# Softplus of the time steps: one VectorE sum out of the bank, the bias as a matmul row, dt written by VectorE

## The chip, the cores and the metric

The kernel runs on one core of one Trainium2 chip. The metric is the device time of one execution in microseconds, as the median of three runs. A profiled execution of the same kernel gives the trace that the sections below read. The engines are called PE (TensorE, with PEld for its weight loads), DVE (VectorE), ACT (ScalarE), POOL (GpSimd) and SP (SyncE, which issues nearly all DMAs here).

## The reference

The input is x of shape (4, 384, 32, 32) in float32: four images, 384 channels, 1024 positions. Two layers follow.

Layer 0 normalises x by groups of channels and runs a selective scan in four directions k (by rows, by columns, and both backwards). For each direction:

```python
dts = jnp.einsum('bkrl,kdr->bkdl', x_dbl[:, :, :R], dt_projs_weight)      # R = 12
dt = jax.nn.softplus(dts + dt_projs_bias[None, :, :, None])
# per position, for each of the 16 states n:
h = h * jnp.exp(dt[..., None] * A) + (dt * u)[..., None] * B
y = einsum(h, C)
```

The four results and a skip term are added up, normalised over channels, put through gelu and added to x. Layer 1 is attention over 1024 positions with a causal window of 64 (six heads of 64), then a mixture of four experts, two per position, with hidden size 1536. All of it is in float32.

The change concerns softplus and the product dt * u. With z = dts + bias and e = exp(-|z|), softplus(z) is max(z, 0) + log(1 + e). The kernel computes the logarithm with a correction for the rounding of w = 1 + e: it takes c = (w - 1) - e and uses log(w) - c.

## The kernel before

**Tiles and turns.** Channels are cut into T = 3 parts of 128 partitions. A turn is one image and one direction: 16 turns. In a turn, each third of the channels has one time step tile of 128 x 1024, so there are 48 steps. For the scan, each third is cut again into four blocks of 32 channels, and each block, with 4 states side by side, gives four tiles of 128 x 1024 called slots: 768 slots in all.

**A slot.** ACT writes the decay dA = exp(dt * A) into PSUM (`decay`, two buffers of two banks). POOL multiplies dt * u by B into z (`times_b`, seven buffers). DVE runs the scan over dA and z (`scan`). The product with C is made on POOL or on DVE (`times_c`), whichever the written order says is less loaded. PE folds the four states into a sum in a PSUM bank (`fold_y`). Attention (`tokens`), routing (`route`) and experts (`experts`, `combine`) of finished images run beside the scan of later ones; what is left of them runs after the last scan.

**Order.** All instructions are written ahead of time. `Machine.run` (line 335) steps through generators such as `time_steps` and `scan`, prices every operation with a simple model (`Engine.ask`, line 154) and appends it to the order of its engine. On the chip each engine runs its own list in that order, and waits where an operand isn't there. Shared buffers are `Stock`s; taking one can have to wait. For PSUM there are the two dA buffers, one bank for the experts' output and the stock `banks` of only three banks (line 471), which everything else shares by rank: 0 for the time steps and the folds, 1 by default, 2 for the experts' hidden layer. `copy` (line 561) puts a copy out of a bank on DVE or ACT, whichever modelled clock is behind.

**A time step before** (`time_steps`, line 741). It may run up to 40 slots ahead of the scan. SP loads u. Two banks are taken, one for each half of 512 columns, and PE multiplies `dtw_sb` (12 rows of weights) by `xd` (12 rows). The halves use rows 0 to 11 and 32 to 43, which `turn_loads` (line 717) has loaded for the turn with two DMAs each. ACT then makes Abs into e and Relu into dt, both with the per-partition bias `dtb_sb`, and the banks are given back. ACT makes Exp over all 1024 columns of e. Two banks are taken anew, and ACT writes w = 1 + e into them. DVE makes c in e. ACT makes Ln in place in the bank. For each half DVE subtracts c, adds dt (both in place in the bank) and multiplies by u into e. ACT copies the bank to dt, and the bank is given back. SP writes e and dt to DRAM (`dtr`), from where `spread` loads them, each row four times over. For directions 1 and 3 the multiply reads u by columns.

The tiles u, e and dt are 128 x 1024 each in SBUF; e and dt have one buffer each, so the next step waits for their DMAs.

Of the kernel before, what the change touches and what calls it, by code (L numbers as in the profile page):

```python
# [11 lines left out]
F32 = mybir.dt.float32  # L12
AF = mybir.ActivationFunctionType
ALU = mybir.AluOpType
# [3 lines left out]
P = 128  # L18
B, D, HH, WW = 4, 384, 32, 32
L = HH * WW  # L20
T = D // P
HB = 512
NH = L // HB
KG, NS, R = 4, 16, 12
# [42 lines left out]
def colmajor(ap):  # L67

    return ap.rearrange("p (h w) -> p w h", w=WW)
# [307 lines left out]
def conv_attn_hybrid(  # L377
# [7 lines left out]
    nc = tc.nc  # L385
    const = ctx.enter_context(tc.tile_pool(name="const", bufs=1))
    dram = ctx.enter_context(tc.tile_pool(name="dram", bufs=2, space=bass.MemoryType.DRAM))

    def const_load(src, shape, name):
        dst = const.tile(shape, F32, name=name)  # L390
        nc.sync.dma_start(dst, src)
        return dst

    xw_sb = const_load(xw, [P, T, KG, XR], "xw_sb")
    dtb_sb = const_load(dtb, [P, KG, T], "dtb_sb")
    ds_sb = const_load(ds_, [P, KG, T], "ds_sb")
    lnw_sb = const_load(lnw, [P, T], "lnw_sb")
    lnb_sb = const_load(lnb, [P, T], "lnb_sb")
# [72 lines left out]
    banks = Stock(m, ps_b, "ps", 3, [P, HB])  # L471
# [4 lines left out]
    with tc.tile_pool(name="setup", bufs=1) as setup:  # L476
# [15 lines left out]
        for j in range(JB):  # L492
            ps = banks.now("ps_al")
# [15 lines left out]
    work = ctx.enter_context(tc.tile_pool(name="work", bufs=1))  # L509
# [42 lines left out]
    pe, act, dve, pool, sp = m.pe, m.act, m.dve, m.pool, m.sp  # L552
# [65 lines left out]
    def group_norm(b):  # L618
# [68 lines left out]
        def project(pair):  # L687
            xos = yield from zs_.take("xo", n=2)
            for h in range(NH):
                us = yield from us_.take("ux", n=2)  # L690
                uv = [us[t // NH][:, ts(t % NH, HB)] for t in range(T)]
                for t in range(T):
                    yield from sp.dma_start(uv[t], udr[b][t][:, ts(h, HB)])
                ps = yield from banks.take("ps_x", 0)
                pv = ps[: 2 * XR, :]
                mm = Calls()
                for t in range(T):
                    mm.matmul(
                        pv, xw_sb[:, t, 2 * pair : 2 * pair + 2, :].rearrange("p k r -> p (k r)"),
                        uv[t], start=t == 0, stop=t == T - 1,  # L700
                    )
                yield from pe.all(mm)
                us_.give(*us)
                yield from act.copy(xos[0][: 2 * XR, ts(h, HB)], pv)
                yield from copy(
                    xos[1][: 2 * XR, :].rearrange("r (w h) -> r h w", h=HH)[:, ts(h, HH // NH), :],
                    pv.rearrange("r (h w) -> r h w", w=WW),
                )
                banks.give(ps)
            for n in (1, 0):  # L710
                yield from sp.dma_start(xdr[b][2 * pair + n], xos[n][n * XR : (n + 1) * XR, :])
                have.add(("x", b, 2 * pair + n))
            zs_.give(*xos)

        yield from m.together([project(pair) for pair in (0, 1)], 2 if b == 0 else 1, EARLY)

    def turn_loads():
        for i, (b, k) in enumerate(turns):
            yield lambda: ("x", b, k) in have and (i == 0 or (i - 1, T - 1) in dtrs)

            xd = work.tile([32 + R, HB], F32, tag="xd", name="xd")
            dtw_sb = work.tile([32 + R, D], F32, tag="dtw", name="dtw_sb")
            for h in range(NH):
                r = slice(32 * h, 32 * h + R)
                yield from sp.dma_start(xd[r], xdr[b][k, :R, ts(h, HB)])
                yield from sp.dma_start(dtw_sb[r], dtw[:, k])
            xds[i], dtws[i] = xd, dtw_sb

    def state_rows(c):
# [11 lines left out]
    def time_steps():  # L741

        for i, (b, k) in enumerate(turns):
            for t in range(T):
                yield lambda: i in xds and ("u", b) in have and count_of["scan"] >= (i * T + t) * TS - 40
                u = yield from us_all.take("ub")
                yield from sp.dma_start(u, udr[b][t])


                e = work.tile([P, L], F32, tag="e", name="e")  # L750
                dt = work.tile([P, L], F32, tag="dt", name="dt")
                bias = dtb_sb[:, k, t : t + 1]
                pss = []
                for h in range(NH):
                    pss.append((yield from banks.take("ps_dt", 0)))
                mm = Calls()
                for h in range(NH):
                    r = slice(32 * h, 32 * h + R)
                    mm.matmul(pss[h], dtws[i][r, ts(t, P)], xds[i][r], start=True, stop=True)
                yield from pe.all(mm)  # L760
                for h, ps in enumerate(pss):
                    c = ts(h, HB)
                    yield from act.activation(e[:, c], ps, AF.Abs, bias=bias)
                    yield from act.activation(dt[:, c], ps, AF.Relu, bias=bias)
                    banks.give(ps)
                yield from act.activation(e, e, AF.Exp, scale=-1.0)

                ws = []
                for h in range(NH):
                    w = yield from banks.take("ps_sp", 0)  # L770
                    yield from act.activation(w, e[:, ts(h, HB)], AF.Identity, bias=1.0)
                    ws.append(w)
                for h, w in enumerate(ws):
                    c = ts(h, HB)
                    yield from dve.scalar_tensor_tensor(e[:, c], w, -1.0, e[:, c], ALU.add, ALU.subtract)
                for w in ws:
                    yield from act.activation(w, w, AF.Ln)
                for h, w in enumerate(ws):
                    c = ts(h, HB)
                    yield from dve.tensor_tensor(w, w, e[:, c], ALU.subtract)  # L780
                    yield from dve.tensor_tensor(w, w, dt[:, c], ALU.add)
                    if k % 2:
                        v = slice(h * (WW // NH), (h + 1) * (WW // NH))
                        yield from dve.tensor_tensor(
                            e[:, c].rearrange("p (w h) -> p w h", h=HH),
                            w.rearrange("p (w h) -> p w h", h=HH), colmajor(u)[:, v, :], ALU.mult,
                        )
                    else:
                        yield from dve.tensor_tensor(e[:, c], w, u[:, c], ALU.mult)
                    yield from act.copy(dt[:, c], w)  # L790
                    banks.give(w)
                us_all.give(u)
                dtr = dram.tile([2, P, L], F32, tag="dtr", name="dtr", bufs=4)
                yield from sp.dma_start(dtr[1], e)
                yield from sp.dma_start(dtr[0], dt)
                dtrs[i, t] = dtr
# [679 lines left out]
    with tc.manual_schedule():  # L1476
        for b in range(B):
            m.spawn(group_norm(b), EARLY)
        for gen in (turn_loads(), time_steps(), state_rows(0), state_rows(1), spread(1), spread(0)):
            m.spawn(gen, EARLY)  # L1480
        for gen in (decay(), times_b(), scan()):
            m.spawn(gen)
        m.spawn(layer1(), EARLY)
        for gen in (prepare(), mixture()):
            m.spawn(gen, LATER)
        m.run()
# [54 lines left out]
```

## Time and profile before

| What | us |
| --- | --- |
| median of three runs | 4074.07 (4067.94 to 4078.49) |
| profiled execution, its own time | 4065.49 |
| its span | 4063.8 |
| POOL's first z product starts | 95.7 |
| last scans end (VectorE's list of instructions in order of time) | about 3140 |
| DVE / POOL / ACT / PE busy in the span | 2878.0 / 2855.7 / 2432.7 / 3014.8 |
| ACT table loads, 388 of 1283 ns | 497.8 |

In the profile's groups, a line names the engine, the operation, "out<-in" with the program's tile names (`ps_dt` and `ps_sp` are the banks of a time step, `ub` is u), the shapes and the count; then busy time, mean length in ns, idle time of the engine just ahead of it and what ended that idle time. L141 and L152 are the helper lines that issue single operations and lists of them, so groups are told apart by tile. In the waits, "A x <- B y: 10.0, 5, 3.0" says that engine A stood still 10.0 us ahead of x, 5 times, at most 3.0 us, until B had made y.

### The profile page before, as it was taken

To read this page: it belongs to the slowest core of one execution; us is meant where nothing else is said; L and a number is where in the kernel's file an instruction comes from. 1 tells how busy PE (TensorE), PEld (TensorE's weight loads), DVE (VectorE), ACT (ScalarE), POOL (GpSimd) and SP (SyncE) were. 2 spreads that over 40 slices of the span, in tenths; PEclk is the share of its full clock that TensorE was granted. 3 is DMA by queue.
4 is the path that set the end of the run, shared out by engine and by line. 5 is a ranking of instruction groups with operands and counts; after the bars stand their busy time and mean duration, and the time that the engine had idled before them with its cause. 6 is when DMAs were issued, how large, how long until landed. Compare 5 with 4: busy or idle time off the path is not lost. (4 is left out here: it accounts for less than half of the span.)

```text
span 4063.8 us, 49234 instructions
## 1 busy us (share of the span) xinstructions
PE 3014.8 (74%) x15856; PEld 1854.0 (46%) x15856; DVE 2878.0 (71%) x3064; ACT 2432.7 (60%) x3979; POOL 2855.7 (70%) x1490
## 2 busy tenths in 40 slices
PE   3554455576674888677777786767799999998998
PEld 1000000043441455445454444444466788887886
DVE  2999999998889888888888889888897232101001
ACT  3554455476774798777776787877777345222221
POOL 1999989989897789999987899899997110101001
PEclk8555566577775899878877787887799999998997
DMA  5565564634345989464668795664569754998995
GB/s 200 203 250 209 217 209 151 209 109 162 114 154 184 382 315 355 164 229 140 215 209 283 268 358 195 230 197 171 190 243 337 240 170 142 345 335 295 315 317 193
DMA packets 368570, 935.11 MB, mean 230 GB/s; under 512 B 48372, under 2 KB 160120, under 8 KB 368312
## 3 DMA queue, kind: packets, MB, share of 16 engines
q1 hardware_dynamic: 360120, 906.79, 63.6%
q0 software_dynamic: 8192, 25.17, 1.8%
q8 instruction: 126, 2.06, 0.2%
q14 instruction: 132, 1.08, 0.1%
HBM read 786.39 MB, written 164.30 MB: 234 GB/s over the span
## 5 line engine op out<-in xcount | busy, mean ns | idle before, releaser
L141 POOL TENSOR_TENSOR z<-dts,bc 128x1024 f32<-128x1024 f32 x768 | 1792.2, 2358 | 177.7 <-PE ps_y L152 95.3
L141 ACT ACTIVATE dA<-dts,a 128x1024 f32<-128x1024 f32 x768 | 851.1, 1116 | 485.5 <-DVE z L141 456.6
L152 PE MATMUL ps_y<-z,fold 128*32 128x512 f32 x3072 | 734.9, 806 | 536.1 <-POOL z L141 253.6
L141 DVE TENSOR_TENSOR_SCAN dA<-dA,z 128x1024 f32<-128x1024 f32 x393 | 899.1, 2288 | 107.6 <-ACT dA L141 88.6
L141 POOL TENSOR_TENSOR z<-z,bc 128x1024 f32<-128x1024 f32 x375 | 879.6, 2356 | 102.6 <-DVE z L141 99.7
L141 DVE TENSOR_TENSOR_SCAN z<-dA,z 128x1024 f32<-128x1024 f32 x375 | 843.8, 2276 | 41.2 <-ACT dA L141 39.4
L152 PEld LDWEIGHTS ps_hid<-xbt,w_sb 128*128 128x128 f32 x5472 | 682.1, 201 | 132.5 <-issue 25.7
L152 PE MATMUL ps_hid<-xbt,w_sb 128*128 128x128 f32 x5472 | 702.0, 286 | 38.0 <-ACT dt L141 19.4
L152 PE MATMUL y_ff<-w_sb,hs 128*128 128x384 f32 x1824 | 659.7, 500 | 19.2 <-ACT hs L141 15.2
L141 ACT ACTIVATE hs<-ps_hid,bb 128x128 f32<-128x128 f32 x912 | 270.5, 366 | 457.1 <-PE ps_hid L152 351.6
L152 PEld LDWEIGHTS ps_y<-z,fold 128*32 128x32 f32 x3072 | 95.1, 123 | 971.4 <-POOL z L141 466.2
L141 ACT ACT_TABLE_LOAD x388 | 497.8, 1283 | 17.2 <-issue 3.6
L141 DVE TENSOR_TENSOR z<-dA,bc 128x1024 f32<-128x1024 f32 x393 | 479.8, 1221 | 13.0
L152 PEld LDWEIGHTS y_ff<-w_sb,hs 128*128 128x128 f32 x1824 | 331.7, 195 | 240.5 <-issue 47.5
L141 POOL DMA_INDIRECT cb<-ysdr,idx x64 | 61.7, 963 | 441.6 <-issue 281.7
L141 DVE COPY xbt<-ps_xb 128x384 f32<-128x384 f32 x39 | 21.7, 556 | 407.7 <-PE ps_xb L152 407.7
L152 POOL TENSOR_TENSOR rn<-rn,half 128x1 f32<-128x1 f32 x96 | 52.5, 547 | 265.6 <-DVE rn L152 256.2
L141 POOL DMA_INDIRECT xsdr<-tks,idx x64 | 63.9, 999 | 168.9 <-DMA xsdr<-tks,idx 119.5
L152 PE MATMUL ps_dt<-xd,dtw_sb 12*128 12x512 f32 x192 | 99.8, 856 | 45.9 <-ACT dt L141 19.2
L152 PE MATMUL ps_o<-v,pt 128*128 128x64 f32 (+1 forms) x720 | 110.1, 315 | 19.6 <-DVE tt L141 7.2
L141 ACT COPY dt<-ps_sp 128x512 f32<-128x512 f32 x96 | 56.0, 584 | 113.5 <-DVE e L141 113.2
L152 PEld LDWEIGHTS ps_o<-v,pt 128*128 128x128 f32 (+1 forms) x720 | 104.9, 227 | 29.4 <-DVE tt L141 7.7
(189 smaller groups left out, 3219.4 us busy)
## 6 DMA issues: line engine op xcount, KB each, us to landing
w_sb<-wl SPq DMA_DIRECT2D x608, 576.0 KB
dts<-dtr SPq DMA_DIRECT2D x384, 512.0 KB
bc<-xdr SPq DMA_DIRECT2D x128, 512.0 KB
ub<-udr SPq DMA_DIRECT2D x48, 512.0 KB
dtr<-e SPq DMA_DIRECT2D x48, 512.0 KB
dtr<-dt SPq DMA_DIRECT2D x48, 512.0 KB
yp<-ydr SPq DMA_DIRECT2D x96, 256.0 KB
ydr<-yp SPq DMA_DIRECT2D x96, 256.0 KB
```

The source lines that it names most:

```text
L141: return getattr(self.real, op)(*a, **k)
L152: getattr(self.real, op)(*a, **k)
```

## The change

z with its bias comes ready out of the matmul, and dt never passes through a bank on its way out.

- The bias becomes a 13th row of the weights, against a row of ones. `xd` is one constant tile, set to 1.0 once, of which the turns overwrite rows 0 to 11 and 32 to 43. Twelve small DMAs at the start lay the bias out in DRAM (`dtbr`), and each turn loads its row twice. `dtb_sb` is gone.
- ACT makes Abs of both halves without a bias, then Exp. There is no Relu.
- DVE makes max(z, 0) + e out of the bank into dt in one instruction.
- ACT writes w = 1 + e over z in the same bank; no second pair of banks is taken. The two banks are held from the matmul to the last subtraction.
- DVE makes (w - 1) - (max(z, 0) + e) in e, ACT makes Ln in place, and DVE subtracts: dt = log(w) - e goes straight to SBUF. The bank is given back there.
- The multiply by u reads dt from SBUF in place of w in the bank. ACT's copy to dt is gone.

```diff
-    dtb_sb = const_load(dtb, [P, KG, T], "dtb_sb")
...
+    xd = const.tile([32 + R + 1, HB], F32, name="xd")
+    nc.vector.memset(xd, 1.0)
+    dtbr = dram.tile([KG, D], F32, name="dtbr", bufs=1)
+    for k in range(KG):
+        for t in range(T):
+            nc.sync.dma_start(dtbr[k, ts(t, P)].unsqueeze(1), dtb[:, k, t : t + 1])
+
     def turn_loads():
...
-            xd = work.tile([32 + R, HB], F32, tag="xd", name="xd")
-            dtw_sb = work.tile([32 + R, D], F32, tag="dtw", name="dtw_sb")
+            dtw_sb = work.tile([32 + R + 1, D], F32, tag="dtw", name="dtw_sb")
             for h in range(NH):
                 r = slice(32 * h, 32 * h + R)
                 yield from sp.dma_start(xd[r], xdr[b][k, :R, ts(h, HB)])
                 yield from sp.dma_start(dtw_sb[r], dtw[:, k])
+                yield from sp.dma_start(dtw_sb[32 * h + R : 32 * h + R + 1, :], dtbr[k : k + 1, :])
...
-                bias = dtb_sb[:, k, t : t + 1]
...
-                    r = slice(32 * h, 32 * h + R)
+                    r = slice(32 * h, 32 * h + R + 1)
...
                 for h, ps in enumerate(pss):
+                    yield from act.activation(e[:, ts(h, HB)], ps, AF.Abs)
+                yield from act.activation(e, e, AF.Exp, scale=-1.0)
+                for h, ps in enumerate(pss):
                     c = ts(h, HB)
-                    yield from act.activation(e[:, c], ps, AF.Abs, bias=bias)
-                    yield from act.activation(dt[:, c], ps, AF.Relu, bias=bias)
+                    yield from dve.scalar_tensor_tensor(dt[:, c], ps, 0.0, e[:, c], ALU.max, ALU.add)
+
+                for h, ps in enumerate(pss):
+                    yield from act.activation(ps, e[:, ts(h, HB)], AF.Identity, bias=1.0)
+                for h, ps in enumerate(pss):
+                    c = ts(h, HB)
+                    yield from dve.scalar_tensor_tensor(e[:, c], ps, -1.0, dt[:, c], ALU.add, ALU.subtract)
+                for ps in pss:
+                    yield from act.activation(ps, ps, AF.Ln)
+                for h, ps in enumerate(pss):
+                    c = ts(h, HB)
+                    yield from dve.tensor_tensor(dt[:, c], ps, e[:, c], ALU.subtract)
                     banks.give(ps)
-                yield from act.activation(e, e, AF.Exp, scale=-1.0)
-
-                ws = []
-                for h in range(NH):
-                    w = yield from banks.take("ps_sp", 0)
-                    yield from act.activation(w, e[:, ts(h, HB)], AF.Identity, bias=1.0)
-                    ws.append(w)
-                for h, w in enumerate(ws):
-                    c = ts(h, HB)
-                    yield from dve.scalar_tensor_tensor(e[:, c], w, -1.0, e[:, c], ALU.add, ALU.subtract)
-                for w in ws:
-                    yield from act.activation(w, w, AF.Ln)
-                for h, w in enumerate(ws):
-                    c = ts(h, HB)
-                    yield from dve.tensor_tensor(w, w, e[:, c], ALU.subtract)
-                    yield from dve.tensor_tensor(w, w, dt[:, c], ALU.add)
...
-                            w.rearrange("p (w h) -> p w h", h=HH), colmajor(u)[:, v, :], ALU.mult,
+                            dt[:, c].rearrange("p (w h) -> p w h", h=HH), colmajor(u)[:, v, :], ALU.mult,
...
-                        yield from dve.tensor_tensor(e[:, c], w, u[:, c], ALU.mult)
-                    yield from act.copy(dt[:, c], w)
-                    banks.give(w)
+                        yield from dve.tensor_tensor(e[:, c], dt[:, c], u[:, c], ALU.mult)
```

## The prediction

> **What bounds the kernel now.** I began with the busy times of the page and split the span where the picture changes. POOL's first product starts at 95.7 us and the last scan ends near 3142 us. The answer by stretches, with columns us, PE, PEld, DVE, ACT, POOL busy, TensorE clock, DMA share, GB/s:
>
> ```profile
> PE 3014.8 (74%) x15856; PEld 1854.0 (46%) x15856; DVE 2878.0 (71%) x3064; ACT 2432.7 (60%) x3979; POOL 2855.7 (70%) x1490
> ...
> 130.00:800.00 670.00, 341.04 (x862) 46.54 (x862) 645.57 (x440) 343.78 (x373) 631.38 (x276) 0.56 0.58 205
> 800.00:3142.00 2342.00, 1751.68 (x9417) 1076.86 (x9418) 2040.50 (x2107) 1759.18 (x2731) 2094.42 (x1060) 0.81 0.64 226
> 3142.00:4063.80 921.80, 877.12 (x5473) 712.89 (x5471) 140.97 (x446) 279.21 (x816) 88.67 (x120) 0.96 0.76 262
> ```
>
> There are three regimes. Up to 800 us only the scan runs: VectorE is 96% busy, GpSimd 94%, ScalarE 51%. From 800 to 3142 us attention and experts run beside it: VectorE 87%, GpSimd 89%, ScalarE 75%, none full, so order and waits matter. The last 922 us are TensorE's (95%). No time step is computed there, so only the amount of expert work left over can change it.
>
> Next, the groups by shape that the change touches, and the waits on both sides of ScalarE over the whole span:
>
> ```profile
> L141 DVE TENSOR_TENSOR e<-ps_sp,ub 128x512 f32<-128x512 f32 x96 | 82.6, 861 | 3.0
> L141 DVE TENSOR_TENSOR ps_sp<-ps_sp,dt 128x512 f32<-128x512 f32 x96 | 67.1, 699 | 3.2
> L141 ACT ACTIVATE dt<-ps_dt,dtb_sb 128x512 f32<-128x512 f32 x96 | 65.9, 687 | 1.0 <-DMA dtr<-dt 1.0
> L141 ACT ACTIVATE e<-ps_dt,dtb_sb 128x512 f32<-128x512 f32 x96 | 65.4, 681 | 29.5 <-PE ps_dt L152 27.2 <-DMA dtr<-e 2.2
> L141 ACT COPY dt<-ps_sp 128x512 f32<-128x512 f32 x96 | 56.0, 584 | 113.5 <-DVE e L141 113.2
> ```
>
> ```profile
> DVE dA L141 <- ACT dA L141: 88.6, 68, 3.8
> DVE z L141 <- ACT dA L141: 39.4, 35, 3.6
> ```
>
> ScalarE stands still 113 us ahead of the copies of dt, and VectorE waits 128 us for decays (dA) from ScalarE. Only 2.0 us of that 128 falls between 130 and 800 us.
>
> Last, VectorE operations whose inputs both lie in SBUF. The kernel has them only in small sizes, in group norm and routing:
>
> ```profile
> L141 DVE TENSOR_TENSOR g<-g 128x3 f32<-128x3 f32 x8 | 8.4, 1056 | 0.2
> L141 DVE SCALAR_TENSOR_TENSOR g<-g 128x3 f32<-128x3 f32 x4 | 7.1, 1778 | 1.0 <-POOL g L141 1.0
> L141 DVE TENSOR_TENSOR g<-g,mv 128x3 f32<-128x3 f32 x4 | 4.9, 1213 | 0.1
> L152 DVE TENSOR_TENSOR ps_r<-p,r 128x32 f32<-128x32 f32 x4 | 4.4, 1103 | 0.2
> L152 DVE TENSOR_TENSOR ps_r<-ps_r,r 128x32 f32<-128x32 f32 x4 | 0.8, 200 | 0.1
> ```
>
> The last two rows are one operation on one shape: 1103 ns with both inputs in SBUF, 200 ns with one in PSUM. The order of time (start, length) shows what it waits for:
>
> ```profile
> 2066.46 2.34 POOL L141 TENSOR_TENSOR z<-dts,bc 128x1024 f32<-128x1024 f32 x1
> ...
> 2068.77 2.33 POOL L141 TENSOR_TENSOR z<-z,bc 128x1024 f32<-128x1024 f32 x1
> 2068.86 2.27 DVE L141 TENSOR_TENSOR g<-g,mv 128x3 f32<-128x3 f32 x1
> 2071.05 2.28 DVE L141 TENSOR_TENSOR_SCAN z<-dA,z 128x1024 f32<-128x1024 f32 x1
> ```
>
> Three elements take 2.27 us and end, at 2071.13, with GpSimd's product (2071.10). The same operation took 0.16 us at 24.9 us, when GpSimd was idle.
>
> **What the Trainium skill says.** "SBUF — State Buffer", section "Who interferes with whom": a VectorE instruction with two SBUF inputs contends with a GpSimd instruction that reads SBUF, one with at most one SBUF input does not. Section "SBUF: two separate sides" adds that whoever starts first has the shared ports for its whole instruction. The trace agrees: the rows above, and the scans (one input in PSUM) that run beside GpSimd at a steady 2.28 us. "ScalarE: Activation LUTs", section "What ACT_TABLE_LOAD costs", puts a per-partition bias at about 93 ns; the trace has 681 to 687 ns with one and 580 ns for the Ln without, so about 100 ns.
>
> **The change part by part.** A step is one of 48 (a turn and a third of the channels), in two halves.
>
> *ScalarE loses work.* Per half the Relu (0.687) and the copy of dt (0.584) go, and Abs loses its bias (0.10): 96 x 1.37 = 132 us, 2.7 us a step. The idle time ahead of the copies, 113 us or 2.4 us a step, goes with them; in its place Identity waits for VectorE's max-and-add, with a decay or other ScalarE work queued behind it if the written order is tight. ScalarE's time itself is on no path that sets the end before 800 us; after it, the decays that VectorE waits for come sooner. Of those 125.7 us (86.7 + 39.0 after 800 us) I take a third, since the softplus burst is about a fifth of ScalarE's work there but comes in one piece: **-42 us**. Bounds: 0 and -100.
>
> *VectorE keeps its count.* Eight operations of 512 a step before, eight after: max-and-add out of the bank replaces the add of dt, and three of the four kinds still have one PSUM input (0.68 to 0.70 us each). No gain, no loss.
>
> *The multiply by u changes its ports.* Before, it reads w in PSUM and u in SBUF (861 ns: 0.68 by rows, 1.03 by columns). After, it reads dt and u, both in SBUF. The trace has no such operation of 512, so I bound it. From the small ones while GpSimd ran: g<-g six times 8.04 us against 1.08 unhindered, g,mv three times 4.74 against 0.48, the scalar form three times 6.94 against 0.48, p,r three times 4.21 against 0.60; 21.3 us over 15, or 1.42 us each. From GpSimd's products: one is under way 88% of the time (2672 of 3046 us) and lasts 2.31 us from start to start, so half of that times 0.88 is 1.0 us; the second multiply of a step comes 0.68 us after the first let go and waits 1.6; mean 1.3. I take 1.4, that is 2.8 us a step and 134 us in all. Lower end 0 (not held at that size), upper 2.3 (always a whole product).
>
> In the 13 steps before 800 us VectorE has 4% to spare, so all counts: 13 x 2.8 = 36 us. In the 33 after that it has 9 us of idle a step (301.5 / 33), but in-order waits rather than free room; I let half vanish: 33 x 1.4 = 46 us. Sum **+82 us**; with nothing hidden it is 129 (46 x 2.8).
>
> *GpSimd in turn is held* for at most the multiply's own 0.69 to 1.03 us, 96 x 0.86 = 83 us. I take 0: its loss comes at moments when VectorE is the later of the two, and they feed each other through seven z buffers. If that cover is missing it is up to +80.
>
> *Banks.* Before, two of the three banks are given back after Relu, taken again for Identity and kept until the dt copy: about 3 us each, then 11 to 12. After, they stay taken from the matmul to the last subtraction: Exp and one more trip to VectorE longer (some 3 us), one add, multiply and copy shorter (0.70 + 0.86 + 0.58, plus 1.2 of waiting). I take 0. If it is worse, expert blocks move into the tail at (362 + 348)/41 = 17.3 us of TensorE each, the tail's ps_hid and y_ff work over its 41 blocks.
>
> *Loads.* SP issues twelve small transfers for the bias rows at the start, about 0.45 us each, 5.4 us. SP otherwise stands from 6.8 to 13.57 us waiting for the set-up, so they are hidden; without that cover 5 us. Their four-byte pieces may delay the x loads by 0 to 5 us; I take 0, as vb_sb has such pieces and cost the same 0.43 us to issue. Each turn adds two rows on SP (32 x 0.5 = 16 us), behind the weights' load, whose wait for the old weights they share; the transfers queued behind on SP come 1 us later. Steps are allowed 40 scans (about 160 us) ahead, so nothing is due; only the first turn shows it, under 2 us, against about as much saved in the first chain. The 13th row of the matmul and the memset of xd cost nothing that the trace can tell; the missing dtb_sb load neither.
>
> Sum: -42 + 82 = **+40 us** on the profiled execution's own 4065.5 us (span 4063.8), so 4105.5. That execution lies 8.6 us under the median of the three runs, so 4074.1 + 40, about **4115**.
>
> **The rivals.**
>
> *Not slower, because ScalarE's relief is worth more than the lock.* For it: VectorE waits 128 us for decays, and the multiplies could fall where it would have waited anyway. Against it: before 800 us there is nothing to relieve. With two thirds of the wait gone (-84), the 36 us of the first stretch and 13 of the 46 after it: 4074 - 35 = 4039. It decides from a held time under 0.7 us a multiply (42 us over 26 + 33 multiplies that count), or a relief over 82 us.
>
> *Nothing is hidden.* The full 129 us and no relief: 4203. For it: both engines near 90%. Against it: the 301 us of VectorE's idle time.
>
> *Banks push experts into the tail.* Two blocks more: 4115 + 35 = 4150. For it: only three banks, and experts take theirs with the lowest rank. Against: the two hold times come out alike.
>
> *No difference.* The order is written from modelled costs that know no lock; VectorE's count is unchanged, and "one sum" replaces one sum. Lock and relief cancel: 4074.
>
> **How the numbers follow.** The forecast's case has 0.45, the full lock 0.10, banks 0.10, the faster rival 0.25, no difference 0.10. A measurement of this kernel tells 0.3% (12 us) from no change. Slower 0.45 + 0.10 + 0.10 = 0.65, same 0.10, faster 0.25. The forecast's own range is 4087 to 4155. The range from 4028 to 4195 takes in most of the faster case and leaves out the upper part of the full lock, about 0.07 to 0.1 at each end.
>
> **What would show it.** The row e<-dt,ub should stand at about 2.2 us (1.9 to 2.6) for 96; at 0.9 the lock is refuted. Rows for Relu and the dt copy are gone, Abs is near 0.58. VectorE's wait for dA should fall from 128 to about 85. The scan part should end near 3180 us and the tail stay near 920. The forecast is wrong if the tail moves by more than two blocks (35 us), if the scan part ends by 3142, or if VectorE gives its copies to ScalarE on a large scale, since copies go to the engine whose clock is behind.

## The result, and the profile after

The changed kernel took 4194.76 us (median of 4 runs, 4188.67 to 4197.59) against 4073.76 us for the kernel before, measured beside it: a ratio of 1.0296, with a 95% interval from 1.0278 to 1.0314. It is slower by 121 us. The forecast was 4115, so the direction was right and the size a third of what came. The profiled executions have spans of 4187.0 and 4063.8 us; what follows explains the 123.2 us between them. Executions of one kernel differ by more than the small terms below: 36 runs of the kernel before lie between 4061.97 and 4087.72 us, and the profiled one took 4065.49. A few us between two profiles therefore tell nothing, and where it matters the medians of the runs stand beside the profiles.

The span falls into three parts: the start up to GpSimd's first z product, the scan part up to the end of the last scan, and the tail.

| us | before | after | difference |
| --- | --- | --- | --- |
| start | 95.7 | 107.9 | +12.2 |
| scan part | 3044.6 | 3136.7 | +92.1 |
| tail | 923.5 | 942.4 | +18.9 |
| VectorE busy in the scan part | 2716.6 | 2835.8 | +119.2 |
| VectorE idle in the scan part | 328.0 | 300.9 | -27.1 |
| all 96 multiplies by u | 82.6 | 208.4 | +125.8 |

The stretch of the scan part before (start and end, length, then PE, PEld, DVE, ACT, POOL busy, TensorE clock, DMA share, GB/s):

```profile
95.70:3140.30 3044.60, 2105.66 (x10315) 1127.67 (x10315) 2716.59 (x2571) 2127.45 (x3134) 2758.43 (x1348) 0.76 0.63 222
```

The busy times of the changed kernel's page, and its stretches, cut where the 192nd of the 768 scans starts and where the last one ends:

```profile
PE 3054.3 (73%) x15844; PEld 1884.5 (45%) x15844; DVE 3002.2 (72%) x3082; ACT 2315.6 (55%) x3765; POOL 2879.5 (69%) x1486
...
107.90:823.80 715.90, 329.45 (x864) 50.36 (x864) 687.44 (x448) 328.00 (x339) 643.98 (x278) 0.57 0.57 195
823.80:3244.60 2420.80, 1802.28 (x9417) 1096.59 (x9418) 2148.32 (x2132) 1686.66 (x2590) 2139.62 (x1068) 0.80 0.63 220
3244.60:4187.00 942.40, 894.79 (x5500) 724.76 (x5498) 143.24 (x452) 276.93 (x811) 88.96 (x119) 0.95 0.76 259
```

In the kernel before, the same cuts give 681.0, 2363.6 and 923.5 us. The stretch up to the 192nd scan thus became 34.9 us longer, and the rest of the scan part 57.2 us. ScalarE lost 117 us of work over the span (2432.7 to 2315.6) and VectorE gained 124 (2878.0 to 3002.2).

The groups of the softplus in the changed kernel:

```profile
L141 DVE TENSOR_TENSOR e<-dt,ub 128x512 f32<-128x512 f32 x96 | 208.4, 2170 | 3.1
L141 DVE TENSOR_TENSOR dt<-ps_dt,e 128x512 f32<-128x512 f32 x96 | 64.9, 676 | 3.4 <-ACT ps_dt L141 3.3
L141 DVE SCALAR_TENSOR_TENSOR dt<-ps_dt,e 128x512 f32<-128x512 f32 x96 | 61.6, 677 | 29.4 <-ACT e L141 29.4
L141 DVE SCALAR_TENSOR_TENSOR e<-ps_dt,dt 128x512 f32<-128x512 f32 x96 | 61.3, 678 | 0.4 <-ACT ps_dt L141 0.2
L141 ACT ACTIVATE e<-ps_dt 128x512 f32<-128x512 f32 x96 | 52.3, 588 | 33.5 <-PE ps_dt L152 27.6 <-DMA dtr<-e 5.8
```

The multiply by u is the one VectorE operation of the softplus whose length changed: 2170 ns, where it took 861 while it read w in the bank. The three others, with an input in a bank, stand at 676 to 678 ns. On ScalarE the Relu and the copy of dt are gone, and Abs without a bias takes 588 ns, 93 less than with one.

The longest waits of VectorE in the scan part, after:

```profile
DVE yp L141 <- PE ps_y L152: 60.0, 38, 8.8
DVE dA L141 <- ACT dA L141: 43.8, 36, 3.3
DVE z L141 <- ACT dA L141: 42.2, 40, 3.4
DVE dA L141 <- POOL z L141: 27.8, 18, 8.6
```

The two waits for decays from ScalarE sum to 86.0 us, where the kernel before had 128. But the waits for a sum from TensorE and for z from GpSimd grew. Before, they were:

```profile
DVE yp L141 <- PE ps_y L152: 39.5, 29, 3.7
DVE dA L141 <- POOL z L141: 12.5, 9, 6.3
```

### The profile page after: what moved, and what is told of

It reads as the page before. It is cut to its first block, busy times and chain, and to the rows that moved or that the text cites. A ratio compares the mean times of both kernels' runs of the same rounds, so it can differ in the third digit from the quotient of the medians.

```text
span 4187.0 us, 49004 instructions
## 1 busy us (share of the span) xinstructions
PE 3054.3 (73%) x15844; PEld 1884.5 (45%) x15844; DVE 3002.2 (72%) x3082; ACT 2315.6 (55%) x3765; POOL 2879.5 (69%) x1486
## 5 line engine op out<-in xcount | busy, mean ns | idle before, releaser
L141 POOL TENSOR_TENSOR z<-dts,bc 128x1024 f32<-128x1024 f32 x768 | 1813.8, 2386 | 207.5 <-PE ps_y L152 118.1
L141 ACT ACTIVATE dA<-dts,a 128x1024 f32<-128x1024 f32 x768 | 851.6, 1116 | 702.4 <-DVE z L141 679.3
L141 DVE TENSOR_TENSOR_SCAN z<-dA,z 128x1024 f32<-128x1024 f32 x371 | 834.0, 2275 | 42.8 <-ACT dA L141 42.2
L141 DVE TENSOR_TENSOR e<-dt,ub 128x512 f32<-128x512 f32 x96 | 208.4, 2170 | 3.1
L152 PE MATMUL ps_s<-k,q 64*128 64x192 f32 (+1 forms) x384 | 92.1, 398 | 49.5 <-DVE mx L141 10.0
L152 PE MATMUL ps_dt<-xd,dtw_sb 13*128 13x512 f32 x192 | 92.8, 809 | 43.5 <-DMA xdr<-xo 16.4
L152 PE MATMUL ps_o<-v,pt 128*128 128x64 f32 (+1 forms) x720 | 107.6, 310 | 17.3 <-ACT tt L141 5.0
```

What stands on the lines that cost most here:

```text
L141: return getattr(self.real, op)(*a, **k)
L152: getattr(self.real, op)(*a, **k)
```

## The experiments

Two questions were open: whether the multiply's longer stay is worth its full length, and what the 42 us are that the forecast gave to ScalarE's relief. "The lock" means the wait of the multiply, with both inputs in SBUF, for ports that GpSimd's products hold; "ScalarE's relief" means the work and the standing still that the change takes from ScalarE. Each expectation names its own theories. "Frozen" means that the instruction lists were written with the costs of the unaltered kernel, so that every engine keeps its order and only what the diff shows is different. This matters because the written order follows from modelled costs, and an edit of an operation would otherwise rewrite the order around it.

**The multiply's ports alone, in the kernel before (`b_lock`).** The order is frozen; the multiply reads dt in SBUF and not w in the bank.

```diff
-yield from dve.tensor_tensor(e[:, c], w, u[:, c], ALU.mult)
...
+yield dve.ask("tensor_tensor", (ev, wv, uv, ALU.mult), {})
+nc.vector.tensor_tensor(ev, dv, uv, ALU.mult)
```

> The kernel before with its written order untouched; only the multiply by u reads dt in SBUF (it holds max(z,0) then) in place of w in the bank, so the logarithm is left out of dt*u. Nothing else changes: no relief on ScalarE, the same banks, the same start. Theory 1 (the lock between VectorE and GpSimd, which hardly anything hides): the 96 multiplies rise from 0.86 to about 2.1 us each, the scan part grows by 90 to 120 us, the start and the tail stay, about 4165 to 4190 us. Theory 2 (the lock is mostly hidden; the rewritten order of the changed kernel, with two banks held longer, costs the time): the multiplies rise as well but the time grows by 20 to 45 us, about 4095 to 4120.

It took 4181.18 us, a ratio of 1.0247 (1.0215 to 1.0278). The group of its multiplies and its scan part as one stretch:

```profile
L791 DVE TENSOR_TENSOR e<-dt,ub 128x512 f32<-128x512 f32 x96 | 194.2, 2023 | 0.0
```

```profile
97.30:3253.53 3156.23, 2133.33 (x10314) 1145.35 (x10315) 2821.67 (x2571) 2127.52 (x3131) 2788.44 (x1348) 0.74 0.61 214
```

The multiplies grew by 194.2 - 82.6 = 111.6 us, and the scan part by 3156.2 - 3044.6 = 111.6 us. That the two agree to the decimal is chance; by the medians the kernel is 105 us longer (88 to 113). After the 192nd scan, where the forecast let half vanish, the multiplies grew by 69.1 us and the stretch by 73.3. VectorE's idle time took up nothing: it is 334.6 us here and 328.0 before. GpSimd's busy time in the scan part rose from 2758.4 to 2788.4 us on the same instructions, so GpSimd seems to be held as well, by some 30 us, but no time beyond the multiplies' own growth shows at the end. The forecast's zero for it stands.

**The lock taken out of the changed kernel (`a_free`).** The order of the changed kernel is frozen. In the multiply's place stands an operation of about the former length with one SBUF input, u; dt is left out of the product.

```diff
-yield from dve.tensor_tensor(e[:, c], dt[:, c], u[:, c], ALU.mult)
...
+yield dve.ask("tensor_tensor", (ev, dv, uv, ALU.mult), {})
+nc.vector.tensor_reduce(ev, ux, AX.X, ALU.add)
```

> The changed kernel with its written order untouched; in place of the multiply dt*u, VectorE passes u alone through an instruction of the same width with one SBUF input, so the factor dt is left out of dt*u. Theory 1 (lock): these instructions fall to 0.7 to 1.1 us, the scan part shrinks by 85 to 115 us and only the later start (12 us) and the longer tail (19 us) remain, about 4080 to 4110 us. Theory 2 (rewritten order and banks): the scan part shrinks by 20 to 45 us, about 4150 to 4175.

It took 4060.64 us, a ratio of 0.9962 (0.9944 to 0.9979).

```profile
L795 DVE TENSOR_REDUCE e<-ub 128x512 f32<-128x512 f32 x96 | 82.9, 864 | 3.1
```

```profile
105.20:3115.71 3010.51, 2102.70 (x10281) 1123.47 (x10282) 2707.17 (x2578) 2012.36 (x2929) 2750.20 (x1345) 0.76 0.64 224
```

These operations take 125.5 us less than the multiplies of the changed kernel, and the scan part is 126.2 us shorter. The lock is the whole of the slowdown, and more: without it the changed kernel lies under the kernel before, below the range in which the first theory put it. Its scan part is 34.1 us shorter than before, with VectorE idle for 303.3 us. So something else in the change saves about 34 us there. The medians agree: the kernel is 15 us under the one before although its start is 9.5 us and its tail 14.0 us longer. The agreement with the Trainium skill is direct: "SBUF — State Buffer", section "Who interferes with whom", lets a VectorE operation with at most one SBUF input, outside its two-port modes, run beside GpSimd, and these take 864 ns, as the multiply out of the bank did (861).

**Is a longer VectorE worth its length whatever makes it longer? (`b_long`).** Every multiply of the kernel before is done twice, out of the bank, in a frozen order. Both times one input lies in PSUM, so no lock is added.

```diff
 yield from dve.tensor_tensor(e[:, c], w, u[:, c], ALU.mult)
+nc.vector.tensor_tensor(e[:, c], w, u[:, c], ALU.mult)
```

(For directions 1 and 3 the second one reads u by columns, like the first.)

> The kernel before with its written order; VectorE makes each multiply by u twice, both times out of the bank, so its work grows by 96 x 0.86 = 83 us with no lock. Theory 1 (in the scan part every microsecond on VectorE is one on the end, whatever it consists of): the scan part grows by 75 to 90 us, about 4150 to 4165. Theory 2 (the lock costs as much as it does because it also holds GpSimd, and plain VectorE time is half hidden in its idle time): the scan part grows by 30 to 50 us, about 4105 to 4125.

It took 4148.37 us, a ratio of 1.0176 (1.0150 to 1.0201).

```profile
L791 DVE TENSOR_TENSOR e<-ps_sp,ub 128x512 f32<-128x512 f32 x48 | 49.2, 1025 | 1.7
L796 DVE TENSOR_TENSOR e<-ps_sp,ub 128x512 f32<-128x512 f32 x48 | 33.2, 691 | 1.6
```

```profile
99.40:3221.84 3122.44, 2132.19 (x10314) 1147.89 (x10315) 2794.19 (x2665) 2127.36 (x3132) 2760.25 (x1349) 0.75 0.61 216
```

The second multiplies, by rows and by columns, are 82.4 us. The scan part grew by 77.8 (3122.4 against 3044.6), and VectorE's idle time is 328.3 us, as it was. So 94% of plain added work came out as time in the profile; by the medians it is 73 us (61 to 82), or 88%. The full price in the runs above is no property of the port; it is VectorE that sets the length of the scan part, idle share or not.

**ScalarE's relief alone (`b_relief`).** In the kernel before, with a frozen order, Relu and the copy of dt work on 16 of 512 columns; most of dt is a constant tile.

```diff
-yield from act.activation(dt[:, c], ps, AF.Relu, bias=bias)
+yield act.ask("activation", (dt[:, c], ps, AF.Relu), dict(bias=bias))
+nc.scalar.activation(dtc[:, c][:, :16], ps[:, :16], AF.Relu, bias=bias)
...
-yield from dve.tensor_tensor(w, w, dt[:, c], ALU.add)
+yield dve.ask("tensor_tensor", (w, w, dt[:, c], ALU.add), {})
+nc.vector.tensor_tensor(w, w, dtc[:, c], ALU.add)
...
-yield from act.copy(dt[:, c], w)
+yield act.ask("copy", (dt[:, c], w), {})
+nc.scalar.copy(dtc[:, c][:, :16], w[:, :16])
```

> The kernel before with its written order; ScalarE's Relu and its copy of dt work on 16 of 512 columns (the rest of dt is a constant), so max(z,0) and dt are left out but for those columns. ScalarE loses 96 x (0.687 + 0.584) us less what 32 short instructions of about 0.25 us leave, some 75 us. Theory 1 (relief is worth about a third of VectorE's wait for decays): the scan part shrinks by 20 to 40 us, about 4035 to 4055. Theory 2 (the gain of the changed order without the lock came from the order and not from ScalarE's relief): within 10 us of 4075.

It took 4067.01 us, a ratio of 0.9981 (0.9968 to 0.9994). Its scan part, and VectorE's waits for decays in it (helper lines have moved down by 12):

```profile
96.80:3141.27 3044.47, 2126.51 (x10314) 1144.36 (x10315) 2721.43 (x2570) 2050.72 (x3131) 2757.93 (x1347) 0.75 0.63 222
```

```profile
DVE dA L153 <- ACT dA L153: 86.8, 64, 3.9
DVE z L153 <- ACT dA L153: 37.6, 36, 3.6
```

ScalarE has 76.7 us less work in the scan part (2127.5 to 2050.7), and the scan part is as long as before to 0.1 us. The wait for decays is 124.4 us against 128. The 76.7 us are two thirds of what the change takes from ScalarE (117 us over the span), and they are worth little in the same order. The medians differ by 9 us (2 to 13), and the profiles can't tell 9 us from none: the one before lies 10 us under the median of the 36 runs beside this one, and this one 4 us over its own median. (The short instructions are 192, not the 32 of the expectation.)

**The copies out of ScalarE's list altogether (`b_nocopy`).** A rival remained: in `b_relief` the short copies still stand in ScalarE's list and make it wait for VectorE's multiply, as before. Here the copies are left out, and dt keeps the Relu's values; the order is frozen.

```diff
-yield from act.copy(dt[:, c], w)
+yield act.ask("copy", (dt[:, c], w), {})
```

> The kernel before with its written order, but ScalarE's copy of w to dt is left out altogether (dt keeps max(z,0), so the logarithm is missing from the decays). ScalarE loses 56 us of work and, unlike in the shortened version, also the 113 us in which it stood still ahead of the copies; a bank comes free with the multiply. Theory 1 (what the changed kernel gains without the lock is this standing still): VectorE's wait for decays falls from 128 to about 90 us and the scan part by 20 to 35 us, about 4040 to 4055. Theory 2 (the gain lies in the rewritten order alone): the scan part stays within 8 us of 3045, the time within 10 us of 4075.

It took 4076.60 us against 4081.63, a ratio of 0.9990 (0.9977 to 1.0004); the scan part is 3047.6 us. VectorE's waits for decays there:

```profile
DVE dA L141 <- ACT dA L141: 92.1, 71, 3.8
DVE z L141 <- ACT dA L141: 41.0, 36, 3.6
```

The waits for decays are 133.1 us, not fewer than 128. The 113 us for which ScalarE stood ahead of the copies went elsewhere on ScalarE: its decays now wait 567.2 us for VectorE to free a buffer, 456.6 in the kernel before. So in the old order the work that `b_relief` takes away is worth 13 us at most, and leaving out the copies, with the standing still ahead of them, nothing that can be measured. What is left for the 34 us that `a_free` shows is the new order that the change led to, the dependences of the softplus that only the changed code has (other trips between ScalarE and VectorE, banks held throughout), or ScalarE's relief in that new order. These were not taken apart.

**The small transfers at the start (`b_start`).** The kernel before, with the twelve transfers into `dtbr` added and their result unused.

```diff
+dtbr = dram.tile([KG, D], F32, name="dtbr", bufs=1)
+for k in range(KG):
+    for t in range(T):
+        nc.sync.dma_start(dtbr[k, ts(t, P)].unsqueeze(1), dtb[:, k, t : t + 1])
```

> The kernel before with the twelve transfers of the bias at the start added and nothing that uses them. Theory 1 (they delay the first loads of x): GpSimd's first product moves from 95.7 to about 108 us and the time grows by about 12 us, to about 4087. Theory 2 (a late start is made up, or the changed kernel starts late for another reason): the time stays within 4 us of 4075.

It took 4085.41 us, a ratio of 1.0023 (1.0013 to 1.0032): 9.8 us. GpSimd's first product starts at 106.9 us, 11.2 later than before, and the scan part is 3048.2 us. So the transfers explain nearly all of the start's +12.2. How they do so is in the changed kernel's order of time, SP's queue first and then VectorE (start, length, what it waited for):

```profile
6.39 10.25 SPq L722 DMA_DIRECT2D dtbr<-in_dtb_dram  x12
16.82 2.89 SPq L141 DMA_DIRECT2D xn<-in_x_dram  x3
```

```profile
29.48 1.29 DVE L141 BATCH_NORM_STATS2 st<-xn 128x6 f32<-128x512 f32 x2 [15.72 <-DMA xn<-in_x_dram]
```

SP needs 10.25 us for the twelve, 0.85 us each on average, and issues the first x loads at 16.82 us, which is 3.3 us later than before (13.57). The first group norm starts at 29.48 us where the kernel before started it at 17.22. Of those 12.3 us, then, 3.3 are issue, and the other 9 are the longer time that the x loads took to land once they had been issued. From 18 to 26 us the DMA engines moved 26 GB/s, and from 28 to 34 us 361. That the twelve transfers cause this, `b_start` shows; by what mechanism their four-byte pieces hold up the x loads, it doesn't.

**The bias laid out ahead of time (`a_row`), and on top of it the product out of the bank (`a_bank`).** The first drops `dtbr` and its twelve transfers; the bias goes into the kernel with a row per direction, so that a turn loads its row straight from the input. The second also lets the last subtraction write into the bank, reads the product from there, and has ScalarE copy dt out, as the kernel before did.

```diff
...
-yield from sp.dma_start(dtw_sb[32 * h + R : 32 * h + R + 1, :], dtbr[k : k + 1, :])
+yield from sp.dma_start(dtw_sb[32 * h + R : 32 * h + R + 1, :], dtb[k : k + 1, :])
...
-        "dtb": _channels(a["L0_conv_dt_projs_bias"]),
+        "dtb": a["L0_conv_dt_projs_bias"],
```

> The changed kernel without its twelve transfers at the start: the bias comes as an input laid out in rows, from which each turn loads its row. Theory 1 (the twelve transfers of four-byte pieces delay the first loads of x, and all that follows is later by that): GpSimd's first product falls back from 107.9 to about 96 us and the time by about 12 us, to about 4183. Theory 2 (steps run far enough ahead that a late start is made up): the start falls back but the time stays within 4 us of 4195.

`a_row` took 4184.28 us, a ratio of 1.0257 (1.0211 to 1.0304), 10 us under the changed kernel. Its first product starts at 96.2 us, as expected, 11.7 earlier. But its runs spread over 30 us, and its profiled execution has a scan part of 3153.0 us, 16.3 longer than the changed kernel's. The multiplies took 226.3 us in it, 17.9 more than in the changed kernel's, which is the scan part's difference again. On the total time the run is inconclusive; it suggests that the time lost at the port depends on how the two engines happen to meet.

```diff
-yield from dve.tensor_tensor(dt[:, c], ps, e[:, c], ALU.subtract)
-banks.give(ps)
+yield from dve.tensor_tensor(ps, ps, e[:, c], ALU.subtract)
...
-yield from dve.tensor_tensor(e[:, c], dt[:, c], u[:, c], ALU.mult)
+yield from dve.tensor_tensor(e[:, c], ps, u[:, c], ALU.mult)
+yield from act.copy(dt[:, c], ps)
+banks.give(ps)
```

> The changed kernel with the bias in rows from an input, the last subtraction in place in the bank, the multiply by u out of the bank, and ScalarE's copy of dt back; Relu, the second pair of banks and the per-partition bias stay gone, and all is computed. Theory 1 (lock and start): multiplies near 0.86 us, about 4060 to 4095 us; what is under 4074 is the worth of ScalarE's Relu and bias. Theory 2 (banks held from the matmul to the end cost the time): they are held even longer here, so 4130 us or more.

`a_bank` took 4050.94 us, a ratio of 0.9933 (0.9913 to 0.9953). So it is 25 us faster than the kernel before, with nothing of the computation left out, and below the range that its first theory gave.

```profile
L141 DVE TENSOR_TENSOR e<-ps_dt,ub 128x512 f32<-128x512 f32 x96 | 82.7, 862 | 3.1
```

The multiply is back at 862 ns, the scan part at 3031.6 us. Here the banks are held longest of all the versions, and no cost of it shows in the scan part; the tail, at 932.3 us, is 10 us under the changed kernel's and 9 over the one before.

**Fewer VectorE operations (`a_plain`).** `a_bank` without the correction for the rounding of 1 + e: ScalarE makes log(1 + e) in SBUF in one operation, and VectorE makes max(z, 0) plus that in the bank.

```diff
+yield from act.activation(e, e, AF.Ln, bias=1.0)
...
-yield from dve.scalar_tensor_tensor(dt[:, c], ps, 0.0, e[:, c], ALU.max, ALU.add)
...
-yield from dve.tensor_tensor(ps, ps, e[:, c], ALU.subtract)
+yield from dve.scalar_tensor_tensor(ps, ps, 0.0, e[:, c], ALU.max, ALU.add)
```

> The multiply out of the bank and the bias in rows, and the logarithm taken as Ln(e + 1) in one pass on ScalarE: max(z,0) + Ln(1+e) is then one VectorE instruction in the bank; the correction for the rounding of 1+e is left out. VectorE loses two of four kinds, 96 x 1.36 = 131 us, ScalarE loses Identity. Theory 1 (VectorE's time counts one for one): about 3910 to 3950. Theory 2 (GpSimd becomes the bound once VectorE is relieved): 3980 to 4030.

It took 3946.00 us, a ratio of 0.9670 (0.9646 to 0.9693). Two of the four kinds of VectorE operation are gone; at the 61.3 and 64.9 us that they take in the changed kernel, that is 126 us. The scan part, at 2920.1 us, is 111.5 shorter than that of `a_bank`. VectorE's busy time fell by only 74 us (2703.2 to 2629.0): the written order, which goes by the modelled clocks, moved 29 products with C from GpSimd to VectorE (368 to 339 there, 400 to 429 here, at 1.22 us each on VectorE). This fits a price of about one for one in this direction too, partly by way of GpSimd. It doesn't show it by itself, as the order was written anew and ScalarE lost its Identity as well.

## Why the prediction was right and wrong

**The multiply's length: right as a mean, in part by luck.** The forecast said about 2.2 us and 1.4 us more than before; it is 2170 ns and 1.31 us more. The mean read from operations of three elements, 1.42 us, carried over to one of 512. The other estimate, from GpSimd's products, had the first multiply of a step wait 1.0 us and the second 1.6; they waited 1.81 and 0.81. That its mean of 1.3 fits is luck: it let each multiply wait for the rest of one product, and the last section shows that a third didn't wait and that some waited for several.

**The first stretch: right.** 36 us in full were forecast for the steps before 800 us. The multiplies there grew from 24.8 to 65.8 us, 41.0, and the stretch up to the 192nd scan from 681.0 to 715.9, 34.9.

**"In-order waits rather than free room; I let half vanish": this is the step that failed.** It counted 46 of 92 us. After the 192nd scan the multiplies grew by 84.7 us (55.8 to 140.5), and in the frozen order of `b_lock` no part of such growth vanished there: 69.1 us of it made that stretch 73.3 us longer. `b_long` gave 54.2 for 55.7 us of plain work in the same stretch. The step's own words were right and its number wasn't: in-order waits are not room. VectorE was idle in the scan part for 328.0 us before, 334.6 with the lock and 328.3 with 82 us of plain work added; in the new order it was idle for 300.9 us with the lock and 303.3 without. Within one order, the idle time stays while the work changes. A likely reason, argued and not shown, is that VectorE waits for results whose makers wait for VectorE: ScalarE stood still for 679.3 us ahead of its decays in the changed kernel until VectorE had freed their buffer (456.6 before), so a VectorE that comes later gets its decay later by as much. Priced in full, the term is 125.8 us where 82 stood: 44 us of the miss.

**ScalarE's relief, -42 us: the size nearly right, the mechanism not borne out.** The sign that the forecast named did appear, VectorE's wait for decays at 86.0 us for "about 85". Yet in the old order ScalarE's relief is not worth that: `b_relief` and `b_nocopy` take away, one at a time, most of the work and the standing still, and the scan part stays at 3044.5 and 3047.6 us. What saves time appeared only with the changed kernel's own order and dependences, 34.1 us by `a_free`. Both parts at once, or the relief in the new order alone, were not tried. The waits of `a_free` show why a fall of 42 us in one wait is no gain of 42 us: with no lock, VectorE waits 58.4 us for sums from TensorE and 32.2 for z (39.5 and 12.5 before), while the waits for decays fell from 128 to 88.3 and those for the softplus's own ScalarE results from 21.4 to 6.2. Seven tenths of the fall came back in the waits for TensorE and GpSimd. The rest of the 34 us is 9 us less busy time and smaller waits.

**The loads, 0 us: wrong by 12.** "vb_sb has such pieces and cost the same 0.43 us to issue" looked at the issue alone. The twelve took 0.85 us each on SP, where they are issued, and held back the landing of x by 9 us more. The forecast's upper bound of 5 us for the four-byte pieces was too low. `b_start` puts the whole at 11.2 us in the profile and 9.8 in the runs.

**GpSimd held, 0 us, and the banks, 0 us: right as far as the scan part shows.** GpSimd's busy time rose by 25.2 us in the scan part (2758.4 to 2783.6), and `b_lock` shows no time from that. In `a_bank` the banks are held longest and the time is the lowest with the same arithmetic. Whether the banks, through the order, have a part in the longer tail is open.

**The tail, "near 920": 942.4, within the two blocks that the forecast allowed.** TensorE has 16 us more to do there (894.8 against 878.8). Six more of the experts' groups that ScalarE makes from `ps_hid` fall into the tail (498 against 492). That is half a block of twelve, or about 9 us by the forecast's 17.3 us a block. `a_free` has the same order, no lock, and 937.5 us; the five versions with the old order have 922 to 928. So most of the +19 goes with the order, not with the lock. What in the order does it stays open, and the forecast's rival of the banks, which expected just such a move of expert work, isn't excluded for it.

Put together: +125.8 for the lock, -34 for order and dependences, +12 for the start, +19 for the tail, 123 us. The profile's miss of 83 us (123 where 40 stood) is thus 44 from the lock (39 of it after the 192nd scan, where the half didn't vanish), 12 from the start, 19 from the tail, and 8 from a saving of 34 in place of 42. Of the rivals, "nothing is hidden" was nearest and named the mechanism; it had a chance of 0.10. "No relief" in it was right about ScalarE, but the new order's gain is missing from it, and so are the losses at the start and in the tail, which nearly make up for that: it lies 8 us above the result at 4203.

## What to carry to other kernels

On a kernel whose VectorE and GpSimd both run near 90%, it can pay to leave one input of each VectorE operation in PSUM: moving a single operand of 96 multiplies into SBUF cost 126 us here. Moving it back gave 4051 us, with most of the change kept and the bias laid out ahead of time. Idle time of an engine that works its list in order is not room: count work that is added to the engine that sets the stage in full, and test it by adding plain work in a frozen order. When a wait shrinks, look which wait grows before calling it a gain, and keep small-piece transfers out of the way of the loads that the first computation needs.

## What was not expected of the hardware

The multiply's wait isn't one product of GpSimd. All 96 by length (ns: shortest, median, longest; first and last start):

```profile
L141 DVE TENSOR_TENSOR e<-dt,ub x96: 683/2122/12708, 96.5 to 3030.9; 128x512 f32<-128x512 f32 x96
```

33 of the 96 take under 1.15 us, that is, they aren't held, and two inputs in SBUF by themselves cost nothing. 51 lie between 1.15 and 3.4 us, which is at most one product and the multiply's own time. 12 take 3.5 us or more, that is, longer than one product accounts for. The longest, in the order of time of VectorE and then of GpSimd:

```profile
2707.77 12.71 DVE L141 TENSOR_TENSOR e<-dt,ub 128x512 f32<-128x512 f32 x1
2720.40 0.68 DVE L141 TENSOR_TENSOR dt<-ps_dt,e 128x512 f32<-128x512 f32 x1
2721.12 0.69 DVE L141 TENSOR_TENSOR e<-dt,ub 128x512 f32<-128x512 f32 x1
```

```profile
2703.78 6.97 POOL L141 TENSOR_TENSOR z<-z,bc 128x1024 f32<-128x1024 f32 x3
2710.70 9.23 POOL L141 TENSOR_TENSOR z<-dts,bc 128x1024 f32<-128x1024 f32 x4
2724.05 2.35 POOL L141 TENSOR_TENSOR z<-dts,bc 128x1024 f32<-128x1024 f32 x1 [4.12 <-PE ps_y L152]
```

The multiply starts at 2707.77 us, within the second of the three products of the first row, and ends only when GpSimd has nothing ready, after the third and four more, which end at 2719.93. Five times GpSimd's next product began while the multiply waited, and the multiply that followed while GpSimd stood still took 0.69 us. The forecast had put the upper end at "always a whole product", 2.3 us; single waits went to 12. The trace of the kernel before had such a case already, and it is one of the 15 operations that the forecast averaged:

```profile
1287.71 4.65 POOL L141 TENSOR_TENSOR z<-dts,bc 128x1024 f32<-128x1024 f32 x2
1287.83 4.56 DVE L141 SCALAR_TENSOR_TENSOR g<-g 128x3 f32<-128x3 f32 x1
```

Three elements, in an operation that takes 0.16 us unhindered, took 4.56 us and ended only with the second of two products. Read for its longest wait, and not only for its mean, that group would have told that one product is no bound. The Trainium skill, "SBUF — State Buffer", section "SBUF: two separate sides", has whoever starts first hold the ports for its instruction; the trace agrees, and adds that being next in time does not make VectorE next in turn.

The second surprise was the start: twelve transfers of 128 pieces of four bytes, 6 KB in all, held x back by 12 us.
